# Moving the dilation's tiles to the other end of SBUF and loading the second layer's first inputs behind an earlier branch

## The chip, the cores and the metric

The kernel runs on one core of a Trainium2 chip. The metric is the device time of one execution in microseconds (us), lower is better, given as the median of several runs. A profiled execution gives, beside its own time, a span and a trace of every instruction. PE is the matrix engine (TensorE), DVE the vector engine, ACT the scalar engine, POOL the general engine (GpSimd), and SP the engine that only issues transfers here. POOL issues transfers too. All transfers run on the core's 16 DMA engines.

## The reference

There are 16 graphs of 1024 nodes with 128 features each. `adj` is a weighted adjacency (16 x 1024 x 1024, about 6% of it filled). Layer 0 is three convolutions in which the edge weights are multiplied by the cosine of the node features. Layer 1 first thins each graph, row by row (the "dilation": which edges are kept depends on what earlier rows removed), and then runs three averaging convolutions, each with a batch norm over all graphs.

```python
h = relu(layernorm(x))
for W, b in layer0:                       # three times
    h = h @ W + b
    nh = h / norm(h)
    h = (adj * (nh @ nh.T)) @ h           # relu but for the last
x = x + h                                 # "x2" in the kernel
h = relu(layernorm(x))                    # "h0" in the kernel
adj_d = adj * dilate(adj > 0, mask)       # sequential over the rows of a graph
for Wr, Wx, b, g, be in layer1:           # three times
    agg = (adj_d @ h) / clip(sum(adj_d, -1), 1)
    out = agg @ Wr + h @ Wx + b
    h = batchnorm(relu(out / norm(out)), g, be)      # over all 16 graphs
x = x + concat(h1, h2, h3) @ Wl + bl
```

## The kernel before

**Blocks.** A graph ("batch" b) is cut into 8 x 8 blocks of 128 x 128. Everything that is symmetric is done once for a row q: the blocks c >= q, and their mirror images, 2 * (8 - q) - 1 blocks in all.

**First part (lines 169 to 773).** Two things run interleaved. `layer0()` (line 406) is a generator that writes out by hand the order of layer 0: two batches alternate, each with three convolutions of eight steps; `products` makes adj times cosine (PE line 311, DVE lines 320 and 323), `turn` transposes the mirror blocks (PE line 340, ACT line 341), `sums` and `sums_back` multiply with the features (PE lines 351 and 365). Each `yield` is a step that carries its estimated PE time. The pieces of `adj` come through `nat` tiles (line 211), and the transposed pieces are stored to `adjT` in DRAM (line 229). `dilation()` (line 512) computes which edges stay, on DVE and ACT mostly, and stores them to `keep` in DRAM (line 710). The loop of lines 744 to 747 deals out layer 0's steps between the dilation's by their estimated times, so that 93% of layer 0 should be done when the dilation ends.

The fast dilation counts the cases that it may have got wrong in `astray`. Lines 749 to 756 turn that into a flag, 0 or 1, that every engine loads into a register. Behind the rest of layer 0 stands a branch (line 769): if the flag is set, the whole dilation is run again in an exact form, which is long. With these inputs it is jumped over.

**The tail.** Lines 767 to 773 run what is left of layer 0, the branch, and the last batch's `residual` (line 379: transposes on PE, then x + h on DVE line 388, then POOL's store of x2) and `next_layer` (line 393: layer norm and relu, then POOL's store of h0). For all other batches these two are called inside `layer0()`. The program's scheduler may move an instruction ahead of others that it doesn't depend on, but none moves across the branch on its engine.

**Second part (from line 776).** The tiles of the first part are given up and those of the second are laid over them. A load into a tile waits until the last reader or writer of what lay there is done. For each batch, `fetch` (line 914) loads the batch's `keep` (8 loads of 256 KB, line 917; two buffers) and its h0 as `hN` (line 919; one buffer). Then for each row q `masked` (line 922) loads the row's blocks, transposed ones from `adjT` (line 925) and plain ones from `adj` (line 929), into `aT{q}` (one buffer for each q); PE transposes keep (line 934), DVE combines it with its own transpose (line 936, `both`) and multiplies the blocks by it (lines 942 and 946). `turn` (line 951) transposes the mirror blocks, and POOL stores the masked row to `adT` in DRAM (line 961). Two rows behind, `follow` (line 965) aggregates (PE line 832). The next batch is fetched behind row 1 (line 988). `hN` is transposed and multiplied by the weights (lines 979, 804 to 806) before the batch's first aggregation. I call this the masking stage. The second and third convolution (line 1041) only load `adT` back into the same `aT{q}` tiles and aggregate. SP issues all loads, in one order; POOL all stores of x2, h0, adjT, keep and adT.

```python
            then = fetch(0)
            for b in range(B):
                kb, hN = then
                hT = pool2.tile([P, NCH, P], F32, tag="hT2", name=f"hT1_{b}")
                transposed(ps_sm, hT, hN, f"h1{b}")
                now = Sums(0, b, hT, 3, 1, ps_a)
                for q in range(NCH):
                    behind.append((now, q, masked(b, q, kb)))
```

Of the kernel before, what the change touches and what calls it, by code (L numbers as in the profile page):

```python
# [8 lines left out]
F32 = mybir.dt.float32  # L9
F16 = mybir.dt.float16  # L10
# [36 lines left out]
def tile_adj_preln_d2(  # L47
# [120 lines left out]

    with ExitStack() as actx:
        pool1 = actx.enter_context(tc.tile_pool(name="a1", bufs=1))  # L170
# [39 lines left out]
        def adj_piece(b, q):  # L210
            Nat[b, q] = nat = pool2.tile([P, NCH, P], F32, tag="nat", name=f"nat_{b}_{q}")
            nc.sync.dma_start(
                nat[:, : NCH - q, :], adj[b][q * P :, q * P : (q + 1) * P].rearrange("(c p) q -> p c q", p=P)
            )
# [16 lines left out]
        class Batch:  # L231
# [147 lines left out]
            def residual(self):  # L379
                b = self.b  # L380
                self.x2 = x2 = pool2.tile([P, NCH, D], F32, tag="tt", name=f"x2_{b}")
                for h in range(NHALF):
                    pt = ps_sm.tile([P, CPH, P], F32, tag="sm", name=f"px_{b}_{h}")
                    for c in range(CPH):
                        nc.tensor.transpose(pt[:, c, :], self.hT[:, h * CPH + c, :], ident)
                    for c in range(CPH):
                        n = h * CPH + c
                        nc.vector.scalar_tensor_tensor(
                            x2[:, n, :], pt[:, c, :], self.rn[:, n : n + 1], self.xb[:, n, :], ALU.mult, ALU.add
                        )  # L390
                nc.gpsimd.dma_start(x2_d[b].rearrange("(c p) d -> p c d", p=P), x2)

            def next_layer(self):
                b = self.b
                h0 = pool2.tile([P, NCH, D], F32, tag="tt", name=f"h0_{b}")
                layernorm_relu(pool2, h0, self.x2, f"l1_{b}")
                nc.gpsimd.dma_start(h0_d[b].rearrange("(c p) d -> p c d", p=P), h0)
# [100 lines left out]
        patt = pool1.tile([P, SLOTS, N + 2], F16, name="patt")  # L498
        nc.gpsimd.memset(patt[:, :, 0:2], 0.0)

        astray = pool1.tile([P, BH], F32, name="astray")
        nc.vector.memset(astray, 0.0)

        def thresholds(x, nm):


            th = pool2.tile([P, 2, BH], F32, tag="th", name=f"th_{nm}")
            nc.vector.tensor_scalar(th[:, 0, :], x, EVENS, None, ALU.add)
            nc.vector.tensor_scalar(th[:, 1, :], x, float(T_DIL), LOW, ALU.is_le, ALU.mult)
            return th[:, 0, :], th[:, 1, :]  # L510
# [6 lines left out]
        def dilate(k, half, exact):  # L517
# [8 lines left out]
            left = pool2.tile([P, BH], F32, tag="left", name=f"left{nk}")  # L526
            rest = pool2.tile([P, BH], F32, tag="rest", name=f"rest{nk}")
            if k == 0:
                nc.vector.memset(left, 0.0)
            rbias = pool2.tile([P, BH], F32, tag="rbias", name=f"rbias{nk}")  # L530
            T = pool2.tile([P, BH, P], F16, tag="T", name=f"T{nk}")
            for i in range(BH):
                b = half * BH + i
                an = pool2.tile([P, N], F32, tag="an", name=f"an{nk}_{i}")
# [4 lines left out]
                if k:  # L539
                    pk = pool2.tile([P, NCH - 1, P], F16, tag="kl", name=f"kl{nk}_{i}")  # L540
                    nc.sync.dma_start(
                        pk[:, :k, :].rearrange("p j q -> p (j q)"), keep_d[b][: k * P, cols], transpose=True
                    )
                    nc.vector.scalar_tensor_tensor(
                        pattern(i)[:, 2 : 2 + k * P],
                        an[:, : k * P],
                        0.0,
                        pk[:, :k, :].rearrange("p j q -> p (j q)"),
                        ALU.is_gt,
                        ALU.mult,  # L550
                        accum_out=left[:, i : i + 1],
                    )
                yield 0.75
                if i % GT == GT - 1:
# [5 lines left out]
                    dT = pool2.tile([P, GT, P], F16, tag="dT", bufs=1, name=f"dT{nk}_{i}")  # L560
# [13 lines left out]
            x0 = pool2.tile([P, BH], F32, tag="x0", name=f"x0{nk}")  # L574
# [5 lines left out]
            Z = pool2.tile([P, BH, P], F16, tag="Z", name=f"Z{nk}")  # L580
            if ends:
                nc.vector.tensor_scalar(Z, T, 0.0, None, ALU.is_equal)
            else:
                found = pool2.tile([P, 1], F32, tag="found", name=f"found{nk}")
                nc.vector.tensor_scalar(Z, T, 0.0, 0.0, ALU.is_equal, ALU.add, accum_out=found)
                nc.vector.tensor_tensor(astray[:, 0:1], astray[:, 0:1], found, ALU.add)
            E = pool2.tile([P, BH, P], F16, tag="E", name=f"E{nk}")
            par = pool2.tile([P, BH], F16, tag="par", name=f"par{nk}")

            def even(x, nm):  # L590

                ev = pool2.tile([P, BH], F32, tag="ev", name=f"ev_{nm}")
                nc.vector.tensor_scalar(ev, x, EVENS, EVENS, ALU.add, ALU.subtract)
                return ev

            def removals(x, nm):


                if exact:
                    f, low = thresholds(x, nm)  # L600
                    at = pool2.tile([P, 2, BH], F32, tag="at", name=f"at_{nm}")
# [8 lines left out]
                else:  # L610
                    ev = even(x, nm)
                    mid = pool2.tile([P, BH], F16, tag="mid", name=f"mid_{nm}")
# [13 lines left out]
            if exact:  # L626
                x = pool1.tile([P, BH], F32, tag="xe", name=f"xe_{nk}")
                nc.vector.tensor_copy(x, x0)
                with tc.For_i(0, P, 1):
                    pc = removals(x, f"e{nk}")  # L630
                    nc.vector.tensor_tensor(x, x0, pc, ALU.subtract)
            else:
                x = x0
                for r in range(ROUNDS[k]):
                    was = x
                    pc = removals(x, f"{nk}_{r}")
                    yield 1.0
                    x = pool2.tile([P, BH], F32, tag="x", name=f"x_{nk}_{r}")
                    nc.vector.tensor_tensor(x, x0, pc, ALU.subtract)
                moved = pool2.tile([P, BH], F32, tag="moved", name=f"moved_{nk}")  # L640
                nc.vector.tensor_tensor(moved, was, x, ALU.not_equal)
                nc.vector.tensor_tensor(astray, astray, moved, ALU.add)
            fin = pool2.tile([P, 3, BH], F32, tag="fin", name=f"fin{nk}")
# [9 lines left out]
            else:  # L653
# [9 lines left out]
                small = pool2.tile([P, BH], F32, tag="small", name=f"small{nk}")  # L663
# [20 lines left out]
            for i in range(BH + 1):  # L684
                if i < BH:

                    pt = pattern(i)
                    ranks[i] = rank = pool2.tile([P, N], F16, tag="rank", bufs=3, name=f"rank{nk}_{i}")
# [13 lines left out]
                kp = pool2.tile([P, N], F16, tag="kp", name=f"kp{nk}_{i}")  # L702
# [64 lines left out]
        while step0():  # L767
            pass
# [3 lines left out]
        batches[-1].residual()  # L772
        batches[-1].next_layer()


    with ExitStack() as bctx:
        res = bctx.enter_context(tc.tile_pool(name="res", bufs=1))
        pool2 = bctx.enter_context(tc.tile_pool(name="b2", bufs=2))
        poolr = bctx.enter_context(tc.tile_pool(name="br", bufs=1))
# [6 lines left out]

        def blocks_of(q, nm):


            return poolr.tile([P, 2 * (NCH - q) - 1, P], F32, tag=f"aT{q}", name=f"aT{q}_{nm}")  # L790
# [118 lines left out]
        with ExitStack() as c1:  # L909
            poolk = c1.enter_context(tc.tile_pool(name="bk", bufs=2))  # L910
# [3 lines left out]
            def fetch(b):  # L914
                kb = poolk.tile([P, NCH, N], F16, tag="kb", name=f"kb_{b}")
                for c in range(NCH):
                    nc.sync.dma_start(kb[:, c, :], keep_d[b][c * P : (c + 1) * P, :])
                hN = pool2.tile([P, NCH, D], F32, tag="hN2", bufs=1, name=f"hN1_{b}")
                nc.sync.dma_start(hN, h0_d[b].rearrange("(c p) d -> p c d", p=P))
                return kb, hN  # L920

            def masked(b, q, kb):
                row = NCH - q
                aT = blocks_of(q, f"1_{b}")
                nc.sync.dma_start(
                    aT[:, :row, :].rearrange("p c q -> p (c q)"), adjT_d[b][q][:, q * P :]
                )
                if row > 1:
                    nc.sync.dma_start(
                        aT[:, row:, :].rearrange("p c q -> p (c q)"), adj[b][q * P : (q + 1) * P, (q + 1) * P :]  # L930
                    )
# [3 lines left out]
                both = poolk.tile([P, NCH, P], F16, tag="both", name=f"both_{b}_{q}")  # L935
# [39 lines left out]
            then = fetch(0)  # L975
            for b in range(B):
# [4 lines left out]
                for q in range(NCH):  # L981
# [5 lines left out]
                    if q == 1 and b + 1 < B:  # L987
                        then = fetch(b + 1)
                    if q == 4 and last is not None:
# [11 lines left out]
        poolc = bctx.enter_context(tc.tile_pool(name="bc", bufs=1))  # L1001
# [28 lines left out]
        def residual(b):  # L1030

            x2 = pool2.tile([P, NCH, D], F32, tag="hN2", bufs=1, name=f"x2f_{b}")
# [8 lines left out]
        for l in (1, 2):  # L1041
            last = None
            then = start2(l, 0)
            for b in range(B):
                now = then
                for q in range(NCH):
                    aT = blocks_of(q, f"{l + 1}_{b}")
# [20 lines left out]
        for b in range(B):  # L1068
# [15 lines left out]
            nc.sync.dma_start(out[b].rearrange("(c p) d -> p c d", p=P), y)  # L1084

# [49 lines left out]
```

## Time and profile before

| what | us |
|---|---|
| median of 3 runs (2895.3 to 2902.11) | 2896.18 |
| the profiled execution | 2901.99 |
| its span | 2900.3 |
| PE busy in the span | 2667.8 (92%) |
| DVE busy | 1937.8 (67%) |
| ACT busy | 1426.8 (49%) |
| POOL busy | 467.5 (16%) |

Times in the profile count from the start of the span. Where they fall: the dilation's last store is issued at 1579.08, layer 0's last aggregation (line 365) ends at 1702, the masking stage's first aggregation starts at 1730.08, its batch norm (line 897) at 2173.3, and the two later convolutions and the output fill the rest. A row of the timeline gives the start, the length, engine, line, operation, output and inputs, shape and count; in brackets stand the idle time of the engine just before and what ended it. "SPq" and "POOLq" are the transfers that SP and POOL issue; the length there is that of the issue, not of the transfer. PEld is PE's loading of weights, which overlaps its products. In the slices each digit is a busy share in tenths in one fortieth of the span.

### The profile page before, as it was taken

Reading aid. Unit: us, or ns where it says so; the run is one execution under the profiler, and the core shown is the slowest. Engines: PE = TensorE matmul, PEld = TensorE weight load, DVE = VectorE, ACT = ScalarE, POOL = GpSimd, SP = SyncE. Lnnn points to the kernel's source line nnn. Section 1 sums busy time; section 2 is a strip of 40 time slices with the busy share of each in tenths; the row PEclk is TensorE's granted clock in tenths of the full one; section 3 lists DMA queues with packets and bytes.
Section 4 is the critical chain, followed back from the end, with each engine's and each line's share of the span. In section 5 each row is a group of like instructions: output and inputs, shape, how many; then the busy total and the mean of one; then the engine's idle time right before and its main releaser. Section 6 shows DMA issues by size and latency. Waiting matters only on the chain. (4 is left out here: it accounts for less than half of the span.)

```text
span 2900.3 us, 52009 instructions
## 1 busy us (share of the span) xinstructions
PE 2667.8 (92%) x18803; PEld 2203.2 (76%) x18803; DVE 1937.8 (67%) x4913; ACT 1426.8 (49%) x4100; POOL 467.5 (16%) x619
## 2 busy tenths in 40 slices
PE   6999999899999998988999979999989999899997
PEld 4666676666666666666676758988979999899996
DVE  3787778877878788779877447777772232355565
ACT  6767667557556566455455323333333333333334
POOL 3111112011111111021011002222220010010101
PEclk9999999999999999999999989999999999999999
DMA  9446357347355475296162049999995656566764
GB/s 282 138 142 215 87 173 238 88 143 209 102 178 166 111 231 158 72 258 188 40 190 96 1 154 409 405 403 387 405 371 174 210 199 208 182 228 231 235 226 136
DMA packets 382236, 585.24 MB, mean 202 GB/s; under 512 B 85201, under 2 KB 266449, under 8 KB 381969
## 3 DMA queue, kind: packets, MB, share of 16 engines
q1 hardware_dynamic: 343280, 425.28, 46.4%
q0 software_dynamic: 38688, 156.53, 14.5%
q8 instruction: 152, 2.49, 0.3%
q14 instruction: 116, 0.94, 0.1%
HBM read 403.44 MB, written 163.58 MB: 196 GB/s over the span
## 5 line engine op out<-in xcount | busy, mean ns | idle before, releaser
L832 PE MATMUL agg<-hw,aT 128*128 128x128 f32 (+1 forms) x6144 | 744.8, 277 | 8.6 <-DVE aT L942 7.3
L832 PEld LDWEIGHTS agg<-hw,aT 128*128 128x128 f32 x6144 | 713.5, 193 | 14.3 <-DVE aT L942 9.7
L311 PE MATMUL pg<-nhT 128*128 128x512 f32 (+3 forms) x1152 | 454.0, 497 | 71.4 <-DVE ew L323 61.3
L351 PE MATMUL po<-ew,hS 128*128 128x512 f32 (+3 forms) x1152 | 455.5, 499 | 8.4 <-ACT hTo L374 4.3
L323 DVE TENSOR_TENSOR ew<-pg,adjA 128x768 f32<-128x768 f32 (+3 forms) x528 | 423.4, 824 | 3.7 <-DVEq L769 3.2
L365 PE MATMUL po<-ew,hS 128*128 128x128 f32 x2688 | 368.2, 277 | 0.0
L365 PEld LDWEIGHTS po<-ew,hS 128*128 128x128 f32 x2688 | 339.8, 193 | 35.5 <-issue 34.0
L341 ACT ACTIVATE ew<-gt 128x512 f32<-128x512 f32 (+1 forms) x480 | 208.7, 465 | 266.8 <-PE gt L340 262.7
L311 PEld LDWEIGHTS pg<-nhT 128*128 128x128 f32 x1152 | 188.8, 192 | 174.2 <-issue 131.3
L689 DVE TENSOR_TENSOR_SCAN rank<-patt 128x1024 f16<-128x1024 f16 x128 | 293.0, 2294 | 0.8
L351 PEld LDWEIGHTS po<-ew,hS 128*128 128x128 f32 x1152 | 195.7, 194 | 99.2 <-issue 68.7
L340 PEld LDWEIGHTS gt<-ident,ew 128*128 128x128 f32 x1344 | 169.6, 144 | 97.9 <-issue 71.1
L320 DVE TENSOR_TENSOR ew<-pg,adjA 128x128 f32<-128x128 f32 x384 | 107.2, 279 | 183.0 <-PE pg L311 143.2
L340 PE MATMUL gt<-ident,ew 128*128 128x128 f32 x1344 | 213.2, 278 | 3.5 <-ACT ew L341 3.2
L882 POOL TENSOR_TENSOR o<-o,rn 128x512 f32<-128x512 f32 x96 | 107.2, 1116 | 651.3 <-DVE rn L881 632.5
L804 PE MATMUL pw<-wrx,hT 128*128 128x256 f32 x768 | 182.4, 392 | 10.4 <-ACT hT L1007 9.7
L806 DVE TENSOR_TENSOR own<-pw,bs 128x256 f32<-128x256 f32 x192 | 81.3, 423 | 152.2 <-ACT hw L805 152.2
L804 PEld LDWEIGHTS pw<-wrx,hT 128*128 128x128 f32 x768 | 147.0, 197 | 33.5 <-ACT hT L1007 10.5
L960 ACT ACTIVATE aT<-pta 128x512 f32<-128x512 f32 (+3 forms) x160 | 71.2, 466 | 203.1 <-PE pta L959 172.2
L861 DVE SCALAR_TENSOR_TENSOR o<-agg,invdeg,own 128x128 f32<-128x128 f32 x384 | 109.7, 344 | 87.1 <-PE agg L832 78.4
L877 ACT ACTIVATE own<-o 128x128 f32<-128x128 f32 x384 | 114.6, 301 | 106.7 <-DVE o L861 106.7
L288 POOL TENSOR_TENSOR hS<-hN,rn 128x1024 f32<-128x1024 f32 x48 | 94.9, 1978 | 398.8 <-DVE rn L157 299.5
(165 smaller groups left out, 3950.1 us busy)
## 6 DMA issues: line engine op xcount, KB each, us to landing
an<-in_adj_dram SPq DMA_DIRECT2D x128, 512.0 KB, 4.7
keep<-kp POOLq DMA_DIRECT2D x128, 256.0 KB, 4.0
kb<-keep SPq DMA_DIRECT2D x128, 256.0 KB, 5.6
aT<-adT SPq DMA_DIRECT2D x32, 960.0 KB, 5.2
aT<-adT SPq DMA_DIRECT2D x32, 832.0 KB, 5.0
aT<-adT SPq DMA_DIRECT2D x32, 704.0 KB, 4.8
aT<-adT SPq DMA_DIRECT2D x32, 576.0 KB, 3.4
xb<-in_x_dram SPq DMA_DIRECT2D x31, 512.0 KB, 4.8
```

The costliest lines, as they stand in the source:

```text
L311: nc.tensor.matmul(pg[:, :n, :].rearrange("p c q -> p (c q)"), lhsT=self.nhT[:, q * P : (q + 1) * P], rhs=self.nhT[:, (q + c) * P : (q + c ...
L320: nc.vector.tensor_tensor(ew[:, 0, :], pg[:, 0, :], place[:, 0, :], ALU.mult)
L323: nc.vector.tensor_tensor(both[0][:, :, off, :], pg[:, own:n, :].unsqueeze(1).to_broadcast([P, 2, n - own, P]), both[1][:, :, off, :], ALU ...
L340: nc.tensor.transpose(pt[:, i, :], ew[:, at + i, :], ident)
L341: nc.scalar.activation(ew[:, at : at + n, :], pt[:, :n, :], AF.Copy)
L351: nc.tensor.matmul(self.po[:, c * P : (c + n) * P], lhsT=self.hS[:, q, :], rhs=ew[:, c - q : c - q + n, :].rearrange("p c q -> p (c q)"), ...
L365: nc.tensor.matmul(self.po[:, q * P : (q + 1) * P], lhsT=self.hS[:, q + n, :], rhs=ew[:, NCH - 1 - q + n, :], start=False, stop=closes and ...
L689: nc.vector.tensor_tensor_scan(rank, pt[:, 1 : N + 1], pt[:, 2:], 0.0, ALU.add, ALU.add)
L804: nc.tensor.matmul(pw[:, i, :], lhsT=hT[:, 2 * h + i, :], rhs=wrx[:, l, :], start=True, stop=True)
L832: nc.tensor.matmul(self.place(c), lhsT=aT[:, blk, :], rhs=self.hw[:, source, :], start=source == 0 and c % self.ga == 0, stop=ends(c, source),
L861: nc.vector.scalar_tensor_tensor(self.o[:, c, :], self.place(c)[:, :P], invdeg[:, b, c : c + 1], self.own[:, c, :], ALU.mult, ALU.add,)
L877: nc.scalar.activation(self.own[:, n, :], self.o[:, n, :], AF.Square, accum_out=ss[:, c : c + 1])
```

## The change

The tiles of the dilation, and the `nat` tiles through which `adj` comes, move from the pools at SBUF's left end into a pool `ad` of their own at the right end. When the dilation's steps have been dealt out, 12 more steps of layer 0 are run, then comes the branch, and then pool `ad` is closed. In its place two pools are opened at the right end: `be` with the tiles of rows 0 and 1, and `bk` with the two keep buffers, `hN`, `both`, and the last batch's x2 and h0. `fetch(0)` and the loads of rows 0 and 1 of batch 0 are called there, ahead of the rest of layer 0 and of the last residual. The last batch's `next_layer` is called only in the masking stage, behind row 3 of batch 0. Rows 2 to 7 stay at the left end. In the later stages `acc` lies at the right end, and the final residual's x2 has a tag of its own instead of sharing the buffer of `hN`. No operation is added or left out.

```diff
+    rctx, kctx = ExitStack(), ExitStack()
+    EARLY = (0, 1)
+    early, kept = {}, {}
+    def row_of(q, nm):
+        pool = kept["early"] if q in EARLY else kept["rows"]
+        return pool.tile([P, 2 * (NCH - q) - 1, P], F32, tag=f"aT{q}", name=f"aT{q}_{nm}")
+    def load_row(b, q):
+        row = NCH - q
+        aT = row_of(q, f"1_{b}")
+        nc.sync.dma_start(aT[:, :row, :].rearrange("p c q -> p (c q)"), adjT_d[b][q][:, q * P :])
+        if row > 1:
+            nc.sync.dma_start(
+                aT[:, row:, :].rearrange("p c q -> p (c q)"), adj[b][q * P : (q + 1) * P, (q + 1) * P :]
+            )
+        return aT
+    def fetch(b):
+        kb = kept["k"].tile([P, NCH, N], F16, tag="kb", bufs=2, name=f"kb_{b}")
+        for c in range(NCH):
+            nc.sync.dma_start(kb[:, c, :], keep_d[b][c * P : (c + 1) * P, :])
+        hN = kept["k"].tile([P, NCH, D], F32, tag="hN2", name=f"hN1_{b}")
+        nc.sync.dma_start(hN, h0_d[b].rearrange("(c p) d -> p c d", p=P))
+        return kb, hN
...
+        poold = dctx.enter_context(tc.tile_pool(name="ad", bufs=2, side="right"))
...
-        while step0():
-            pass
+        for _ in range(12):
+            step0()
         with tc.If(n_off > 0):
             for _ in dilation(exact=True):
                 pass
-        batches[-1].residual()
-        batches[-1].next_layer()
+        assert not Nat
+        dctx.close()
+        kept["early"] = rctx.enter_context(tc.tile_pool(name="be", bufs=1, side="right"))
+        kept["k"] = kctx.enter_context(tc.tile_pool(name="bk", bufs=1, side="right"))
+        ahead1 = fetch(0)
+        for q in EARLY:
+            early[q] = load_row(0, q)
+        while step0():
+            pass
+        batches[-1].residual(kept["k"])
...
             def masked(b, q, kb):
                 row = NCH - q
-                aT = blocks_of(q, f"1_{b}")
...
+                aT = early.pop(q, None)
+                if aT is None:
+                    aT = load_row(b, q)
...
-            then = fetch(0)
+            then = ahead1
...
                     if q == 1 and b + 1 < B:
                         then = fetch(b + 1)
+                    if q == 3 and b == 0:
+                        batches[-1].next_layer(poolk)
...
-        poolc = bctx.enter_context(tc.tile_pool(name="bc", bufs=1))
+        poolc = rctx.enter_context(tc.tile_pool(name="bc", bufs=1, side="right"))
...
-            x2 = pool2.tile([P, NCH, D], F32, tag="hN2", bufs=1, name=f"x2f_{b}")
+            x2 = pool2.tile([P, NCH, D], F32, tag="x2", bufs=1, name=f"x2f_{b}")
```

## The prediction

> **What bounds the kernel now.** I read first the slices of the span, which show where TensorE is not full, then the stretches around the one dip (busy time by stretch), then the timeline inside it, and last what the two queues that matter waited for.
>
> The slices (72.5 us each):
>
> ```profile
> PE   6999999899999998988999979999989999899997
> PEclk9999999999999999999999989999999999999999
> DMA  9446357347355475296162049999995656566764
> ```
>
> PE is at 9 nearly everywhere. Slice 23 (1668 to 1740 us) holds the dip, with a lower clock in it. DMA stands at 0 in slice 22, just before it, and at 9 for the six slices behind it: an idle resource, and then a stage that is short of it. The stretches (us, busy time and instructions of PE, PEld, DVE, ACT, POOL; then granted clock, DMA share, GB/s):
>
> ```profile
> 1620.00:1640.00 20.00, 19.88 (x118) 14.94 (x117) 9.46 (x24) 7.57 (x27) 1.90 (x1) 1.00 0.00 1
> 1700.00:1720.00 20.00, 10.64 (x44) 8.01 (x43) 6.38 (x30) 7.00 (x16) 1.93 (x4) 0.74 0.38 123
> 1720.00:1740.00 20.00, 13.94 (x99) 11.94 (x100) 7.81 (x10) 1.85 (x4) 1.11 (x2) 0.74 1.02 384
> 1760.00:1780.00 20.00, 19.09 (x175) 18.53 (x174) 14.56 (x37) 6.99 (x23) 5.69 (x9) 1.00 1.04 408
> ```
>
> In the first layer's tail (1600 to 1685) DMA moves nothing and DVE is half free. From 1720 to about 2165 all DMA engines are busy at about 405 GB/s: the masking stage runs at DMA's pace. Its bytes agree, from the sizes in the issue table: for each batch keep 8 x 256 KB, hN 512 KB, 36 blocks of 64 KB from adjT, 28 from adj, 64 out to adT, 11.0 MB in all; at the stage's pace (27.9 us a batch: 13 batches between keep's loads at 1751.31 and 2114.35) that is 394 GB/s. SP's queue waits most for room that a store has to clear:
>
> ```profile
> SPq L925 <- DMA adT<-aT: 110.7, 58, 5.2
> ```
>
> The hand-over in the timeline:
>
> ```profile
> 1702.00 1.02 ACT L374 ACTIVATE hTo<-po 128x1024 f32<-128x1024 f32 x1 [3.41 <-PE po L365]
> 1703.82 2.16 DVE L388 SCALAR_TENSOR_TENSOR x<-px,rn,xb 128x128 f32<-128x128 f32 x8 [7.15 <-ACT hTo L374]
> 1706.17 6.65 SPq L919 DMA_DIRECT2D hN<-h  x2
> 1712.48 0.89 POOL L397 DMA_DIRECT2D h<-h  x1 [5.16 <-ACT h L148]
> 1718.45 3.67 SPq L917 DMA_DIRECT2D kb<-keep  x8
> 1730.08 2.92 PE L832 MATMUL agg<-hw,aT 128*128 128x129 f32 x12 [0.38 <-issue]
> ```
>
> The last product ends at 1702. The last batch's residual and norm end in a store issued at 1712.48; the first keep rows go out only at 1718.45, when that store has left the space they need; the first aggregation starts at 1730.08. Twelve us of DMA and some 25 us of PE are lost between two stages, the second of which is short of DMA.
>
> **The change part by part.** Sums are made on the profiled run (2901.99 us, span 2900.3), 5.8 us above the median of 2896.18; I take the saving over unchanged.
>
> *Loads moved ahead.* Behind the branch, 12 steps into the tail, SP issues keep of batch 0 (8 DMAs), hN, and two loads each for rows 0 and 1. A half layer of the tail takes 27.84 us (hS at 1609.82, 1637.66, 1665.50) in some 45 steps, so 12 steps are about 8 us and the loads go out near 1590 to 1600. SP has nothing else to issue from 1582 to 1706, so nothing queues behind its wait. Keep has two buffers, both in the new group, so batch 1's keep can follow too; batch 1's hN waits for the transposes of batch 0's. The bytes taken out of the full stage: 2 x 2.10 MB keep and 1.84 MB rows (1792 KB), 6.03 MB; hN of batch 0 lay ahead of the full stretch already. At 405 GB/s that is **14.9 us**. The Trainium skill, "DMA: Bandwidth & Descriptors" (Where 436 GB/s comes from), lets HBM transfers be bound near 358 GB/s per core, which would make it 16.8 us; the trace holds 403 to 411 for 200 us, so I use the trace. What covers the early loads is the tail with DMA at 0.00; without it they would cost these 14.9 us again.
>
> *Start of the full stretch.* Rows 2 to 7 stay at the left end, over the first layer's buffers. Their last reader is the residual's DVE row, done at 1705.98, and neither norm nor store comes between. From 1718.45 to 1706.0: **12.4 us** earlier.
>
> *What is now late.* The last batch's norm moves into the masking stage, behind row 3 of batch 0: 8 statistics pairs (about 0.43 us a pair by the rows), three short operations and 8 activations (3.19 us): 4 us of DVE and 3.5 us of ACT, beside a stage in which they are busy 14.6 and 7.0 of 20 us. Its store goes on POOL's queue between the stores of adT; those behind it wait some us at most once. But three transfers that lay ahead of the full stretch now fall into it: the residual's and the norm's store and batch 1's hN, 1.57 MB or **3.9 us** back.
>
> *The branch.* It moves from a point with 17 us of work behind it to one with about 113:
>
> ```profile
> L769 PEldq COMPARE_BRANCH  x1: 3867/3867/3867, 1682.2 to 1682.2; - x1
>   DVE ew L323: 3.2, 1
>   PE po L351: 1.2, 1
> ```
>
> PE's sequencer stood for 3.87 us, PE idled 1.23 for it and 1.26 more for DVE: 2.5 us. "Runtime: NRT & Kernel Launch" (Instruction fetch mechanics) speaks against a branch among work: a target outside the prefetched window stops the engine for a fetch. The row is such a stop, but it is paid before too. Bounds of the move: 2.5 us gained if PE's queue covers it, 4.6 lost if PE and DVE stand one after the other (3.87 + 3.24 less 2.5). I take 0, the nearest row being this same branch amid the same mix.
>
> *Placing, tags, later stages.* Other addresses with the same instructions: 0. If a tag made a new wait it would be one DMA latency, 4 to 8 us (issue table); if one falls away, as x2's shared buffer with hN does, nothing is gained, since PE is full from 2180 on. I take 0.
>
> Sum: 14.9 + 12.4 - 3.9 = **23.4 us**. A check by PE instead of bytes: residual to 1706, transposes 1.04, copy 0.6, 16 products 3.72 (at full clock), so hw near 1711.5. By its rows DVE needs 22.7 us for batch 0 (residual 2.2, both 3.6, masks 10.9, own 1.7, sums 4.3), and 4 more if the moved norm comes before batch 1: from 1704 to 1727 or 1731. Batch 1's transposes ran at 1752.09 before: 21 to 25 us. The two agree, and in a stage of even pace a lead lasts to its end, whichever engine sets the pace.
>
> **The rivals.**
> *Only half of it.* SP's queue is in order. If batch 1's hN stands ahead of batch 1's keep and of row 2 (before, an hN went ahead of the first keep), keep 1 (5.2 us) is not early, and the row loads start some 4 us later. 23.4 - 9.2 = 14.2 us: **2882**. For it: that order before. Against: keep 1's buffer is free 100 us earlier than hN's.
> *More than that.* With hN and keep there, transposes and masks of rows 0 and 1 (6 us of DVE) can run inside the tail, where DVE is half free, and PE never cools: batch 0 ends near 1720, a lead of 32 us: **2864**. Against: that lead needs bytes, and bytes allow 23.
> *No gain.* The branch or the freed space comes so late that the loads wait as before. Even a branch at 1687 leaves 19 us for 16 us of loads; only a new dependence on the tail's last reader does it: **2896**.
> *Slower.* No work may cross the branch. With 113 us of two interleaved batches behind it instead of 17, the order of that tail may lose its overlap of PE and DVE, four half layers at 27.84 us. It outweighs the saving from 5.9 us a half layer; at 8.5 us each it gives 34 - 23.4 = 10.6 us: **2907**. Against: DVE and ACT have half of the tail free, and the stop at 1685 was made up within 4 us.
>
> **How the numbers follow.** Forecast 0.62, half 0.16, more 0.12, no gain 0.05, slower 0.05. The predicted time is 2896.2 - 23.4 = 2872.8 us. The forecast's own range is +-7 (branch -2.5 to +4.6, start of the stretch 1702 to 1710). For 8 in 10 it reaches to most of both neighbours: 2860 to 2886. A measurement here tells about 0.3% (8.7 us) from no change; faster by more than that 0.90, within 0.05, slower 0.05.
>
> **What would show it.** Right: keep loads issued before 1620, DMA no longer 0 in slice 22; no stop for keep or adjT between 1700 and 1730; first aggregation near 1712; the first batch norm (2173.3 before) 20 to 27 us earlier; the tail's end still near 1702; PE's clock without the 0.74. Wrong: a second keep only after 1706 (half), half layers longer than 27.84 behind the branch (slower), or a pace above 27.9 us a batch, which would eat the lead.

## The result and the profile after

The changed kernel took 2886.73 us (median of 20 runs, 2879.59 to 2897.28) against 2896.56 us (20 runs, 2887.95 to 2902.11) for the kernel before on the same chips: ratio 0.9971, 95% interval 0.996 to 0.9981. That is 0.3%, 8 to 10 us, where 23.4 were forecast. The profiled execution took 2886.45 us, its span is 2884.7 us. In the traces the stretch from layer 0's last `hTo` copy to the first batch norm went from 471.3 to 457.9 us, 13.4 less, where 20 to 27 were to be seen; behind that batch norm both kernels need 727 us.

What the change sets out to do is all there. The order in which SP issues, in the timeline of the kernel after (start, length of the issue, engine, line, transfer, count):

```profile
1585.58 3.68 SPq L194 DMA_DIRECT2D kb<-keep  x8
1589.30 0.43 SPq L196 DMA_DIRECT2D hN<-h  x1
...
1592.97 7.08 SPq L194 DMA_DIRECT2D kb<-keep  x7
```

Keep of batch 0, hN, rows 0 and 1 (the left-out lines) and keep of batch 1 go out from 1585.58 on; before, the first keep went out at 1718.45. In the slices, slice 22 (counted from 0; 1587 to 1659 us) holds these loads and is no longer empty: DMA stands at 2 where it was 0. Slice 23, PE's dip, is at 8 where it was 7, and its clock at 9 where it was 8:

```profile
PE   6899999899999999988998989999989999899997
PEclk9999999999999999999999999999999999999999
DMA  9447257347355475297063249999985666576764
```

The branch, in its line's own view (duration min/median/max, first and last start), with who waited for it:

```profile
L802 PEldq COMPARE_BRANCH  x1: 3401/3401/3401, 1579.6 to 1579.6; - x1
...
  DVE ew L353: 5.4, 1
  ACT ew L374: 3.3, 1
  PE gt L373: 2.4, 1
```

PE stood 2.4 us for it. From the product that makes the flag (`pf`, at 1578.7 before and 1576.5 after) to the last `hTo` copy it is 123.3 us in both kernels: the tail neither gained nor lost.

The hand-over, in the timeline of after:

```profile
1699.79 1.02 ACT L407 ACTIVATE hTo<-po 128x1024 f32<-128x1024 f32 x1 [3.41 <-PE po L398]
1701.56 2.16 DVE L421 SCALAR_TENSOR_TENSOR x<-px,rn,xb 128x128 f32<-128x128 f32 x8
1703.97 0.33 SPq L183 DMA_DIRECT2D aT<-adjT  x1
1709.26 0.39 PE L868 MATMUL agg<-hw,aT 128*128 128x129 f32 x2
```

Row 2's load leaves at 1703.97, right behind the residual, and the first aggregation starts 9.5 us after the `hTo` copy; before it was 28.1. The DVE row of the residual no longer waits 7.15 us: batch 0's first `both` (DVE, 1700.29) runs just ahead of it. What the lead is worth in bytes, by stretches counted from the last `hTo` copy (the 120 us ahead of it, the first 20, the next 180; busy times of PE, PEld, DVE, ACT, POOL, then granted clock, DMA share, GB/s). Kernel before:

```profile
1582.00:1702.00 120.00, 117.00 (x654) 84.50 (x653) 53.86 (x134) 37.45 (x114) 8.92 (x6) 1.00 0.04 11
1702.00:1722.00 20.00, 8.97 (x35) 6.93 (x35) 6.38 (x30) 7.00 (x16) 1.93 (x4) 0.74 0.43 144
1722.00:1902.00 180.00, 167.27 (x1412) 155.94 (x1411) 128.63 (x299) 64.30 (x218) 41.66 (x67) 0.97 1.04 405
```

Kernel after:

```profile
1579.80:1699.80 120.00, 117.02 (x658) 84.59 (x658) 53.86 (x134) 37.49 (x114) 8.95 (x6) 1.00 0.19 65
1699.80:1719.80 20.00, 17.66 (x153) 16.43 (x150) 15.38 (x42) 8.99 (x21) 2.69 (x6) 1.00 0.77 263
1719.80:1899.80 180.00, 165.41 (x1417) 156.69 (x1416) 131.80 (x321) 66.91 (x229) 46.26 (x72) 0.98 1.03 390
```

The first two rows give a lead of 6.5 + 2.4 = 8.9 MB, 22 us at 405 GB/s. The third gives a part of it back: at 390 in place of 405 GB/s for 180 us it is 2.7 MB, 6.7 us, although the DMA engines count as full in both.

And there is a wait that was not there before:

```profile
1713.88 0.37 SPq L1058 DMA_DIRECT2D x2f<-x  x1
1718.36 2.62 PE L868 MATMUL agg<-hw,aT 128*128 128x129 f32 x22
1725.20 0.87 DVE L1060 SCALAR_TENSOR_TENSOR x2f<-blb,mf,x2f 128x128 f32<-128x128 f32 x3 [7.87 <-DMA x2f<-x]
1726.00 0.41 DVE L959 TENSOR_TENSOR both<-pkb,kb 128x512 f16<-128x512 f16 x1
1727.84 0.88 PE L982 MATMUL pta<-ident,aT 128*128 128x128 f32 x3 [6.69 <-issue]
1728.51 1.71 PE L868 MATMUL agg<-hw,aT 128*128 128x129 f32 x7
```

L1060 belongs to the final residual, which belongs to the last convolution: the load for batch 1 starts only at 2511.75. Before, x2's tile shared hN's buffer, and batch 0's load went at 2145.5. With a tag of its own it is free from the start, and the scheduler set the load of x2 for batch 0 right behind batch 0's last row, and the first DVE operation on it ahead of the masks of batch 0's row 4. The load took 11.3 us to land (median of the 16: 5.0). DVE stands for it, row 4's `both` comes behind it at 1726.00, and PE stops for 6.69 us (the row names no releaser; e1 and e8 below show the cause). The stop costs more than its length: the granted clock, 1.00 ahead of it, was 0.50 from 1727.84 to 1731.80, and a product of L868 took over 0.2 us in the row at 1728.51 where it took 0.12 at 1718.36. Four us at half speed are about 2 us, an estimate; with the stop that makes the 8.8 us that batch 0 loses in the table below.

### The profile page after: what moved, and what is told of

Same layout as the page of the kernel before. It is cut to its first block, busy times and chain, and to the rows that moved or that the text cites. A ratio compares the mean times of both kernels' runs of the same rounds, so it can differ in the third digit from the quotient of the medians.

```text
span 2884.7 us, 52007 instructions
## 1 busy us (share of the span) xinstructions
PE 2661.2 (92%) x18803; PEld 2196.4 (76%) x18803; DVE 1937.6 (67%) x4913; ACT 1427.3 (49%) x4100; POOL 468.7 (16%) x619
## 5 line engine op out<-in xcount | busy, mean ns | idle before, releaser
L868 PE MATMUL agg<-hw,aT 128*128 128x128 f32 (+1 forms) x6144 | 742.9, 277 | 8.2 <-DVE aT L965 7.2
L868 PEld LDWEIGHTS agg<-hw,aT 128*128 128x128 f32 x6144 | 712.6, 192 | 13.3 <-DVE aT L965 9.7
L344 PE MATMUL pg<-nhT 128*128 128x512 f32 (+3 forms) x1152 | 457.2, 500 | 70.7 <-DVE ew L356 60.2
```

Source lines behind the costliest of these rows:

```text
L344: nc.tensor.matmul(pg[:, :n, :].rearrange("p c q -> p (c q)"), lhsT=self.nhT[:, q * P : (q + 1) * P], rhs=self.nhT[:, (q + c) * P : (q + c ...
L868: nc.tensor.matmul(self.place(c), lhsT=aT[:, blk, :], rhs=self.hw[:, source, :], start=source == 0 and c % self.ga == 0, stop=ends(c, source),
```

## The experiments

Three times are read from each trace: when PE starts the transposes of hN (`pt_h`) of batches 1, 2 and 15, counted from the last `hTo` copy, and the length of the stage, from that copy to the first batch norm. Each is one execution, read to about 0.1 us. Before the tail all these kernels issue the same instructions in the same order (but for a few at the very start), and yet they reach it between 1568.8 and 1582.2 us; the stage is free of that. The medians are not, and 4 to 22 runs leave them open by 2 to 5 us. A ratio is taken against the kernel before as it ran beside that run (medians 2896.4 to 2897.7).

| run | median us | ratio, 95% interval | batch 1 | 2 | 15 | stage |
|---|---|---|---|---|---|---|
| before | 2896.56 | 1 | 50.1 | 77.5 | 436.2 | 471.3 |
| after | 2886.73 | 0.9971 (0.996 to 0.9981) | 35.5 | 62.1 | 423.0 | 457.9 |
| e1 | 2892.64 | 0.9987 (0.9979 to 0.9995) | 26.7 | 57.8 | 416.3 | 457.7 |
| e3 | 2887.81 | 0.9966 (0.9953 to 0.998) | 37.3 | 63.9 | 423.4 | 458.3 |
| e4 | 2882.85 | 0.9951 (0.9938 to 0.9964) | 34.6 | 61.2 | 424.1 | 459.0 |
| e6 | 2870.03 | 0.9911 (0.9896 to 0.9926) | 34.8 | 61.4 | 407.9 | 442.8 |
| e8 | 2883.74 | 0.9958 (0.9941 to 0.9975) | 26.7 | 63.9 | 421.7 | 456.7 |
| e9 | 2895.99 | 0.9995 (0.9987 to 1.0002) | 50.7 | 78.6 | 432.5 | 467.4 |
| e10 | 2890.26 | 0.997 (0.9959 to 0.9982) | 27.7 | 63.7 | 422.0 | 456.9 |
| e11 | 2877.97 | 0.9936 (0.992 to 0.9952) | 26.8 | 61.9 | 421.6 | 456.6 |
| e12 | 2863.73 | 0.9881 (0.9866 to 0.9896) | 26.7 | 53.3 | 399.7 | 434.6 |
| e13 | 2883.69 | 0.9956 (0.9942 to 0.9969) | 26.8 | 59.3 | 422.5 | 457.5 |
| e14 | 2890.78 | 0.998 (0.9965 to 0.9994) | 34.7 | 67.4 | 427.4 | 462.3 |
| e15 | 2903.28 | 1.0021 (1.0012 to 1.0029) | 51.6 | 79.7 | 442.3 | 476.9 |
| e16 | 2882.61 | 0.9951 (0.9937 to 0.9965) | 26.8 | 60.2 | 419.1 | 454.1 |
| e17 | 2876.71 | 0.9937 (0.9923 to 0.9952) | 33.1 | 59.7 | 414.0 | 449.0 |
| e18 | 2885.07 | 0.9966 (0.9956 to 0.9976) | 26.7 | 61.8 | 424.1 | 459.0 |

### x2's wait, the norm, the branch, the bytes

The theory was that x2's wait takes the missing 9 us; the rivals, that the norm in batch 0, the place of the branch or DMA's bytes do.

**e1**: x2's tile comes from a pool opened only behind the masking stage.

```diff
-            x2 = pool2.tile([P, NCH, D], F32, tag="x2", bufs=1, name=f"x2f_{b}")
+            x2 = poolc.tile([P, NCH, D], F32, tag="x2", bufs=1, name=f"x2f_{b}")
```

> The changed kernel, but the final residual's x2 tile lies in the group that opens after the masking stage, so its load and its eight additions cannot run inside that stage. Theory (DVE stood 7.87 us in batch 0 for the x2 load that the tag of its own let ahead, and PE 6.69 us with it): the wait goes, keep of batch 2 is issued 5 to 8 us earlier than 1734.5, and the median falls from about 2887 to 2879 to 2882. Rival (the DMA engines were full through that wait at 402 to 417 GB/s, so DVE only waited in their shade): the wait moves to DVE's next load, keep of batch 2 within 2 us of before, median 2886 to 2888.

Batch 0 now ends at 26.7, a lead of 23.4 us over the kernel before (24.0 over e9, which is the kernel before but for the order of the last sum). But nothing of the 8.8 us reaches the end. Batch 1 takes 31.1 us, and at the stage's end the wait is there again (waits in 2140 to 2170, total, times, longest):

```profile
PE pt_r L165 <- POOL o L918: 10.4, 2, 7.5
...
DVE x2f L1060 <- DMA x2f<-x: 6.2, 1, 6.2
```

DVE stands 6.2 us for x2 just where the last batch's norms are due, POOL behind it and PE behind POOL. The wait was moved and not removed, so this run could not settle what it is worth. (Its median is 5.9 us above that of after with the same stage; in the traces the difference lies ahead of the stage, where the instructions are the same: the copy comes at 1705.70 against 1699.79.)

**e3**: the last norm back in the tail, right behind the residual.

```diff
+        batches[-1].next_layer(kept["k"])
...
-                    if q == 3 and b == 0:
-                        batches[-1].next_layer(poolk)
```

> The changed kernel, but the last batch's norm and its store follow its residual at once, as before the change. Rival theory (the 4 us of DVE and 3.2 us of ACT that the norm takes among batch 0's masks are what the hand-over lost): median 4 us lower, about 2883. Main theory (the x2 wait is the loss): the wait of DVE stays, the norm only trades places with batch 0's first masks, median 2885 to 2889.

Stage 458.3 against 457.9: where the norm stands is worth nothing.

**e4**: all of layer 0 ahead of the branch; the loads only behind it.

```diff
-        for _ in range(12):
-            step0()
+        while step0():
+            pass
...
-        while step0():
-            pass
```

> The changed kernel, but all of layer 0's steps come before the branch, as before the change; keep, hN and the two rows are still loaded behind it, now from about 1688. Theory (the branch costs the same 2.3 to 2.5 us of PE at either place, and 16 us of loads still fit before 1705): median within 3 us of the changed kernel's 2887. Rival 1 (an earlier branch costs the tail more): 3 to 6 us lower. Rival 2 (the loads now run into the hand-over): 5 to 10 us higher, with PE waiting for keep or adjT behind 1700.

Tail 123.2 and stage 459.0, as in after. The loads fit into what is left behind a late branch. The median is 4 us below that of after; with e8's edit in both (e10 against e8) the same move gave 6.5 us more. It has no steady sign, and I take it for the spread of the runs.

**e6**: keep is loaded for batch 0 only and used for all batches, which leaves out 15 x 2.1 MB and with it the right keep of the other batches.

```diff
+        if b == 0:
+            kb = kept["kb0"] = kept["k"].tile([P, NCH, N], F16, tag="kb", bufs=2, name=f"kb_{b}")
...
+        kb = kept["kb0"]
```

> The changed kernel, but keep is loaded for batch 0 only and used for all 16 batches: 15 x 2.1 MB of loads are left out. If DMA sets the masking stage's pace, 31.5 MB at 400 GB/s are 79 us: a batch takes near 23 us and the median is 2810 to 2825. If the chain of PE, DVE and ACT within a batch sets it (the last batch before, without keep to load behind it, still took 27 us), a batch stays at 26 to 27 us and the median is 2860 to 2880.

A fifth of the bytes is gone and the stage is only 15 us shorter. From batch 1 on each batch takes 26.65 us, to a few hundredths. Its stretch, and then that of after:

```profile
1800.00:1900.00 100.00, 97.36 (x846) 92.45 (x844) 76.39 (x186) 39.78 (x137) 27.82 (x43) 1.00 0.94 337
```

```profile
1800.00:1900.00 100.00, 94.31 (x824) 89.41 (x822) 74.49 (x180) 38.11 (x130) 26.70 (x41) 1.00 1.04 398
```

PE is at 97% at 337 GB/s, at 94% at 398. So PE's chain alone takes 26.65 us a batch, and with all of keep's loads a batch takes some 27.7 (13 batches of after in 360.9 us). Whether keep adds that 1 us by its bytes or by its place in SP's queue, this run does not tell. A DMA share of 0.94 does not say that DMA sets the pace.

### x2's operations held back by their order

**e8**: the final residual takes up `acc` first and the bias last, the same sum in another order. Its DVE operations then depend on the last aggregation and can't be moved forward; the load still comes early, but nobody waits for it.

```diff
-                    x2[:, c, :], blb[:, 0, :], mf[:, b, c : c + 1], x2[:, c, :], ALU.mult, ALU.add
+                    x2[:, c, :], a, mf2[:, b, c : c + 1], x2[:, c, :], ALU.mult, ALU.add
...
-                nc.vector.scalar_tensor_tensor(a, a, mf2[:, b, c : c + 1], x2[:, c, :], ALU.mult, ALU.add)
+                nc.vector.scalar_tensor_tensor(a, blb[:, 0, :], mf[:, b, c : c + 1], x2[:, c, :], ALU.mult, ALU.add)
```

> The changed kernel, but the final residual adds x2 to acc first and the bias second, so its DVE work depends on acc and cannot run before the last stage; the x2 load stays where it is. Theory (a DVE wait for x2, first in batch 0 and in the kernel with the x2 tile behind the stage at the stage's end, took 7 to 8 us of the lead): neither wait is there, from layer 0's last copy to the first batch norm 449 to 453 us (457.9 in the changed kernel, 457.7 with the tile behind the stage), median 2877 to 2882. Rival (the lead is used up by DMA, whatever DVE waits for): 456 to 459 us, median 2885 to 2890.

The wait is gone and batch 0 ends at 26.7. Yet the stage is 456.7: batch 1 takes 37.2 us. In the timeline of e8:

```profile
1729.99 0.32 SPq L183 DMA_DIRECT2D aT<-adjT  x1
1730.42 5.85 SPq L194 DMA_DIRECT2D kb<-keep  x8
1736.67 0.38 SPq L196 DMA_DIRECT2D hN<-h  x1
1737.30 3.02 SPq L185 DMA_DIRECT2D aT<-in_adj_dram  x1
1749.29 0.69 DVE L969 SCALAR_TENSOR_TENSOR aT<-aT,both 128x512 f32<-128x512 f32 x1 [8.67 <-DMA aT<-in_adj_dram]
1750.08 1.08 PE L982 MATMUL pta<-ident,aT 128*128 128x128 f32 x4 [8.14 <-DVE aT L969]
1750.96 4.89 PE L868 MATMUL agg<-hw,aT 128*128 128x129 f32 x22
```

The two halves of row 3 of batch 1 are loaded by L183 and L185. Between them SP issues keep of batch 2 and its hN, 2.6 MB that no one needs for another 25 us. DVE has the second half only at 1749.29, and PE stops for 8.14 us. The clock was 0.50 in the 5 us behind this stop (0.22 us a product in the last row), about 2.5 us more by the same estimate; together that is what batch 1 takes above 26.6. The theory that x2's wait alone took the missing gain fell here.

**e9** is the kernel before with the same reordered sum.

> The kernel before with the same new order of the final residual and nothing else. It has no wait for x2 in the masking stage, only 2.8 us of DVE in its last batch, so the theory expects 471 to 468 us from layer 0's last copy to the batch norm and a median 0 to 3 us lower than before. If the new order by itself gains more than 5 us, what the run with it on the changed kernel gains is not the wait.

The medians show no difference, as it should be. Its stage is 467.4 against 471.3: batches 2 to 14, in which the two kernels do the same, took 353.9 and 358.7 us. So the stage itself varies by some 4 us from one execution to another.

**e10** is e8 with e4's late branch, **e11** is e8 with the last norm behind row 3 of batch 8 (`if q == 3 and b == 8`).

> The changed kernel with the new order of the final residual and with the branch behind all of layer 0's steps. If the branch's place is worth nothing, as the traces of both places show (123.2 and 123.3 us from the flag's product to layer 0's last copy), the median is within 3 us of the run with the new order alone; if the 4 us by which the late branch came out lower were its own, 3 to 6 us lower than that run.

> The changed kernel with the new order of the final residual and with the last batch's norm behind row 3 of batch 8 instead of batch 0. Its 4 us of DVE then fall into a batch at even pace. If the norm among batch 0's first masks costs anything of its own, batch 1's first transpose comes 2 to 4 us earlier against layer 0's last copy and the median is 2 to 4 us lower than with the new order alone; by the theory (the norm put back in the tail changed the stage by 0.4 us) within 2 us.

Both have e8's stage within 0.2 us. e11's median was the lowest so far of those that leave nothing out; e18 below did not bear it out.

### Keep's place in the queue, or its bytes

**e12** is e8 with e6's single keep; it leaves out the same loads.

> The final residual's reordered sum of e8, and keep is loaded for batch 0 only and used for all batches (15 loads of 2.1 MB are left out, so the output is another one). In e8 batch 1 lost some 10 us because its rows stood in SP's queue behind keep of batch 2. If that queue is the cause, the loss is gone: first batch done at 26.7 us after the last hTo copy, second at about 53.4, each further one 26.65 later, and the stage (last hTo copy to first batch norm) is about 434 us against 442.8 in e6; median about 2861. If batch 1 is slow for another reason than keep's bytes, it stays near 37 us and the stage near 443; median about 2870.

Batch 0 ends at 26.7, batch 1 takes 26.6, and those behind it 26.65 on the mean, to the end: stage 434.6. With keep's loads away no batch is stopped. So they cause batch 1's stop. Against e6, which has the same loads and still has x2's wait in batch 0, the stage is 8.2 us shorter (442.8 to 434.6): with nothing behind it to take the gain again, x2's wait is worth its 8.8 us nearly whole. (The kernel before without keep's loads was not run, so a lead over it can't be given.)

**e13** is e11 with the next batch fetched behind row 5, **e15** the kernel before with that edit.

```diff
-                    if q == 1 and b + 1 < B:
+                    if q == 5 and b + 1 < B:
```

> e11 (x2 order, last norm behind row 3 of batch 8), and the next batch's keep and h0 are fetched behind row 5 and not behind row 1; same bytes. If the order in SP's queue is what takes the lead in batch 1, that batch takes 27 to 31 us and not 35, the lead over the kernel before stays near 20 us, the stage is 449 to 452 us and the median 2871 to 2874. If the bytes are what counts, in whatever order, the stage stays at 456 to 457 and the median at 2878. If keep then comes too late at each batch's start, the pace goes above 27.7 us a batch and it is slower than e11.

> The kernel before with the next batch's keep and h0 fetched behind row 5 and not behind row 1. Control for e13: if that edit has a worth of its own (a pace other than 27.7 us a batch), it shows here; if it only saves the lead, this is the kernel before, 2896, within 4 us, stage 467 to 471.

Batch 1 takes 32.5 us against 35.1 in e11, so a part moved, but the stage is 457.5. The control suggests why not more: the late fetch costs the kernel before 6.7 us by the medians and 5.6 by the stage, so what it gives in batch 1 it seems to take in the pace. This pair did not decide.

**e14** is the changed kernel with `EARLY = ()`: rows 0 and 1 are loaded like the others.

> The changed kernel, but rows 0 and 1 of batch 0 are not loaded ahead and their tiles lie with the other rows; keep and h0 are still early. By the sum of the prediction this costs the 1.84 MB of the rows, 4.5 us of the stage (462.5 against 457.9), median about 2891. If the lead is cut by waits in batches 0 and 1 anyway (for x2f, and for rows behind keep), less is lost: 0 to 2 us, median about 2887.

The stage is 462.3 against 457.9 and the median 4.1 us higher: 4.4 us for 1.84 MB, where the prediction's price of a moved byte gives 4.5. That agrees, but a single stage varies by as much, so it is no proof of the price. The loss shows at the end of batch 1 (67.4 against 62.1), not of batch 0.

### The same bytes in another order

**e16** is e1's and e8's edit together.

> e1 and e8 together: the final residual's x2 tile lies in a pool opened after the masking stage, so its load can't come in batch 0 or at once behind it, and its sum is reordered so that DVE doesn't take it up early. If the 0.5 MB of that load ahead of batch 1's rows is a part of what batch 1 loses, batch 1 takes 31 us as in e1 and not 37 as in e8, the last batch starts at 416 and, with no wait for x2f at the end, the stage is 451 us, median about 2876. If keep of batch 2 in SP's queue does it alone, batch 1 stays near 37 us, the stage at 457 and the median at 2883.

Batch 1 takes 33.4 us, between the two expectations, and the stage is 454.1. That does not price x2's 0.5 MB: from the last copy to the end of batch 1 all engines of e1 and e16 do the same in the same order, and yet batch 1 takes 31.1 and 33.4, so its length varies by 2 us by itself. e11 and e18 differ there in the load of x2 alone, and batch 1 takes 35.1 in both: no cost of that load shows.

**e17** is e16 with a third keep buffer in place of the early rows (there is no room for both). So 6.3 MB of keep are loaded ahead in place of 6.03 MB of keep and rows, and keep of batch 2 is no longer in SP's queue amid batch 1's rows.

```diff
-    EARLY = (0, 1)
+    EARLY = ()
...
-        kb = kept["k"].tile([P, NCH, N], F16, tag="kb", bufs=2, name=f"kb_{b}")
+        kb = kept["k"].tile([P, NCH, N], F16, tag="kb", bufs=3, name=f"kb_{b}")
```

> e16 with three keep buffers and without the early rows: 6.3 MB of keep are loaded ahead in place of 4.2 MB of keep and 1.84 MB of rows, so the bytes ahead are nearly the same, but keep of batch 2 no longer stands in SP's queue ahead of batch 1's rows. If the queue's order takes the lead, batch 0 ends some 4 us later (31), batch 1 then takes 26.7 to 28 and batch 2 starts at 58, the stage is 446 to 450, median about 2872. If bytes alone count, the stage is that of e16 within 2 us, and what batch 1 keeps is lost in the batches behind it.

Batch 0 ends later (33.1, rows 0 and 1 are not there), but batch 1 takes 26.6 us, and the stage is 449.0. In the timeline of SP between the halves of a row there is now only hN:

```profile
1731.61 0.32 SPq L183 DMA_DIRECT2D aT<-adjT  x1
1733.33 0.37 SPq L196 DMA_DIRECT2D hN<-h  x1
1733.74 0.77 SPq L185 DMA_DIRECT2D aT<-in_adj_dram  x1
...
1741.35 6.05 SPq L194 DMA_DIRECT2D kb<-keep  x8
```

And the stretch of 180 us behind the first 20, at 401 GB/s where after had 390:

```profile
1719.20:1899.20 180.00, 169.67 (x1459) 160.29 (x1458) 133.22 (x323) 69.17 (x239) 46.85 (x73) 1.00 1.04 401
```

So with keep of batch 2 out of the way batch 1 isn't stopped, as in e12. But what it saves there, 6.8 us, is little more than the 6.3 that batch 0 lost without its early rows: with nearly the same bytes ahead, batch 2 starts at 59.7, in e16 at 60.2. Up to there the order only moved the loss. The stage is 5.1 us shorter than in e16 because of the batches behind, 2 to 14, which take 354.3 us against 358.9; these vary from 353.9 (e9) to 363 (e13) over all kernels with keep's loads, and the third buffer changes the queue in all of them. That order counts beside bytes is therefore suggested and not shown. The median of 2876.71 us is the lowest of those that leave nothing out, 10.0 us below that of after and 19.9 below that of before, but its interval overlaps those of e11 and e16; the traced stage is 22.3 us shorter than before's and 18.4 shorter than e9's.

**e18** is e16 with e11's norm.

> e16 with the last norm behind row 3 of batch 8, as in e11. By the traces the place of the norm was worth nothing in the stage (456.7 and 456.6), by the medians 5.8 us. If the traces are right, stage and median are those of e16 within 2 us and 4 us. If the norm in batch 0 has a cost, it is 4 to 6 us below e16 again, about 2870.

Median 2885.07 against e16's 2882.61, stage 459.0 against 454.1: not faster. The norm's place has no cost that these runs show, and e11's low median is not a gain of that edit.

## Why the prediction was wrong

Its direction was right and the loads moved as forecast, the size was not: 23.4 us forecast, 13.4 in the traced stage (9.5 against e9's stage of the kernel before), 9.8 by the medians. In the kernel as changed the step that failed is the term "Placing, tags", put at 0: it was 8.8 us in batch 0. The lead at batch 1 was 14.6 us, and from there it held: 15.4 at batch 2, 13.2 at batch 15. A second step, that a lead lasts, would have failed without the first.

*Loads moved ahead, 14.9 us.* Right. The loads left at 1585 to 1600, keep of batch 1 among them, so the rival "Only half of it" did not happen, although the time came out near its 2882. e14 agrees with the price of a byte. (The rates were read a little high: 1720 to 2165 had 398 GB/s on the mean, and 403 to 411 held for 180 us; at 398 the term is 15.1.)

*Start of the full stretch, 12.4 us.* Right: row loads start 4.2 us behind the last `hTo` copy, forecast 4.0. Twenty us behind that copy the lead was 8.9 MB, 22 us at 405 GB/s.

*The branch, 0.* Right: tail of 123.3 us in both. The slower rival didn't happen, nor did "No gain". "More than that" didn't either: DVE's first mask started at 1703.63, behind the residual's adds and not inside the tail.

*The norm in the masking stage.* Right as to its cost: none was seen in e3, e11 and e18.

*"Placing, tags, later stages."* Here it failed. "If a tag made a new wait it would be one DMA latency, 4 to 8 us ... I take 0." It did make one, of 7.87 us on DVE; PE stopped for 6.69 and then ran some 4 us at half clock, and batch 0 ended at 35.5 us where 26.7 were to be had (e1, e8): 8.8 us. The size had been named, the chance that it comes had not been weighed. I had asked what the removed sharing of hN's buffer could gain, not what it had held back. The shared buffer was what kept a load and its DVE operations out of the busiest place in the kernel.

*"In a stage of even pace a lead lasts to its end."* From batch 1 on this held in the changed kernel, but as a step it is wrong too, and without the first failure it would have been the one to cost the lead. With x2's wait away the lead at batch 1 is the forecast 23.4 us (to the tenth by luck), and at batch 2 it is 13.6 (e8), 17.3 (e16) or 19.7 (e1). The stage is not of even pace at its start: PE's chain at 26.65 us a batch runs ahead of what SP has issued, keep of batch 2 goes out between two row loads, and a row comes 8 us late. Without keep's loads (e12) no batch is stopped, down to the last one. With keep of batch 2 loaded earlier (e17) batch 1 is not stopped either, and of its lead of 17.0 us at batch 1 nothing is lost at batch 2 (17.8). In the changed kernel x2's wait came first and batch 1 then took 26.6 us; the two losses don't add, and so taking away the first gave only 1.2 us of the stage in e8 (457.9 to 456.7).

*"The masking stage runs at DMA's pace."* Too simple. It is 1 us a batch above PE's own 26.65. I read the full DMA row as the only limit; e6 shows it nearly full, 0.94, with 15% fewer GB/s.

Still open: how much of batch 1's loss is order and how much bytes. e12 shows that keep's loads make it, but takes their bytes away with their place; e17 keeps the bytes, and is level with e16 at batch 2. A version with the early rows and a third keep buffer was not tried for want of room.

## What to carry to other kernels

A buffer that two tiles share is also an order: before giving a tile a buffer of its own, ask which loads and operations it has kept back, and where a scheduler will put them. When a stage is to start earlier, follow the queue of loads for its first two rounds: what is prefetched for the round after next stands, in an in-order queue, ahead of what the engines need now. A DMA row near full says that transfers are under way, not that they set the pace; take some bytes away and see. And to price a stop of PE, add the products behind it that run at the lower clock.

## What the runs showed of the hardware

A transfer can land much later in a full stretch: x2's first 512 KB took 11.3 us behind batch 0's row loads in after, where the 16 loads of that kind have a median of 5.0. The engines' busy share doesn't follow the rate: 0.94 at 337 GB/s (e6), 1.04 at 398 (after). Behind a stop of PE the granted clock was half for some us: 0.50 from 1727.84 to 1731.80 in after (stop of 6.69 us) and from 1750.08 to 1755.08 in e8 (8.14 us), 1.00 again in 1731.80 to 1740 and 1757 to 1762. And the same instructions in the same order, up to the tail, ended within 1568.8 to 1582.2 us over these runs.
